# Routed expert blocks: one scatter of whole rows per block, or two scatters of half the columns each

## The chip, the core and the metric

The kernel runs on one core of a Trainium2 chip. Its engines are TensorE (PE in the profile, with its weight loads as PEld), VectorE (DVE), ScalarE (ACT), GpSimd (POOL) and SyncE (SP); data moves by 16 DMA engines that all of them share. The metric is the device time of one execution in microseconds; smaller is better. Everything is float32.

## The reference

One decoder layer on x (4 sequences of 512 tokens, 512 wide): a state-space mixer, attention over a context, and a mixture of experts, each behind a layer norm and added to x. The change lies in the last part:

```python
def _L0_ffn_ref(hidden_states, gate_w, expert_bias, ...):   # E = 16 experts, F = 256, K = 2
    x = hidden_states.reshape(-1, h)
    scores = jax.nn.sigmoid(x @ gate_w)
    _, selected = jax.lax.top_k(scores + expert_bias[None, :], K)
    top_scores = jnp.take_along_axis(scores, selected, axis=1)
    top_scores = top_scores / (top_scores.sum(-1, keepdims=True) + 1e-20)
    shared = jax.nn.silu(x @ shared_gate_w) * (x @ shared_up_w) @ shared_down_w
    comb = jnp.zeros((T, E)).at[jnp.arange(T)[:, None], selected].add(top_scores)
    for e in range(E):
        g, u = jnp.split(x @ experts_gate_up[e], 2, axis=-1)
        routed = routed + comb[:, e:e + 1] * (jax.nn.silu(g) * u @ experts_down[e])
    return (shared + routed).reshape(b, s, h)

x = x + _L0_attn_ref(_layernorm(x), ...)
x = x + _L0_xattn_ref(_layernorm(x), ctx_512, ctx_512)
x = x + _L0_ffn_ref(_layernorm(x), ...)
```

## The kernel before

**Up to 1175 us.** The mixer of one sequence and the attention of another are interleaved on TensorE, and the shared expert and the routing of the first three sequences are computed beside the attention of the last. What is left at the end of the attention is the last sequence's norm, its router and the rest of the shared expert. Each 128-token tile of `x + shared` is stored to `out` (`out_x` in the profile, 2176 rows of 512: 2048 tokens and 128 spare rows); the normed tokens go to a DRAM tile `h_d`.

**The routing's result.** `tables()` (L1180 on) makes a table of blocks. Every expert's chosen tokens are cut into blocks of 128 slots; a block belongs to one expert. For block k, `row_i[:, k]` holds the token's row in `h_d` and in `out` for each of the 128 slots (a spare row for an empty slot), and `wslot[:, k]` the token's weight. The last step before it is returned is L1208, `row_i = none - 1`, from a float tile `none` that holds the row plus 1.

**The routed blocks.** `blocks(0, NB_FEW)` runs 42 blocks (`NB_FEW` = 42; five more stand behind a branch and are not needed for these inputs). TensorE's and SyncE's order is as written; the other engines' instructions are ordered by the framework, each engine in order. For each block:

- `gather(k)` (L1340): GpSimd issues an indirect DMA that fetches the 128 rows of `h_d` into one of four places in `res`, as soon as the transposes of the block that had the place before are done.
- `turn_in` (L1350, L1352): four transposes on TensorE, copied by VectorE to `xT`.
- `up` (L1358, L1363, L1365): eight matmul rows in the profile against the expert's gate and up weights, silu on ScalarE, product `actb` on VectorE.
- `turn_act` (L1371, L1373): two transposes, copied by ScalarE to `aT`.
- `down` (L1379, L1384, L1385): four matmul rows into a PSUM bank `pob`, VectorE scales it with `wslot` into `y` (128 x 512, one of three buffers), and GpSimd issues an indirect DMA that adds the 128 rows of `y` to `out` (`compute_op=ALU.add`: each row is read, added and written by the DMA).

In the emitted order on TensorE a block's `down` comes after the next block's `up` and `turn_in`.

**What orders the scatters.** Two blocks may add to the same row of `out` (a token has two experts), so the framework makes each scatter wait for the landing of the one before: GpSimd waits on that DMA's semaphore ahead of the instruction. On GpSimd, in this order: scatter of block k, gather of block k+7, scatter of block k+1 (the first seven gathers stand ahead of the first scatter). `no_dep` tells the framework that two instructions which seem to touch the same memory need no order.

**The expert weights.** A ring of five places (`ring`, `NW` = 5) holds the weights of five experts, 1.5 MB each. Five are loaded before the blocks begin; `load_later` (L1285) fetches the next one when a place is free and skips the load if the next block needs no new expert. All is issued by SyncE on its own DMA queue; gathers and scatters are on GpSimd's queue.

Of the kernel before, what the change touches and what calls it, by code (L numbers as in the profile page):

```python
# [11 lines left out]
I32 = mybir.dt.int32  # L12
AF = mybir.ActivationFunctionType
ALU = mybir.AluOpType
# [3 lines left out]
P = 128  # L18
B, L, D = 4, 512, 512
# [15 lines left out]
NB = 2 * NT + E - 1  # L35
# [4 lines left out]
ROWS = B * L + P  # L40
# [8 lines left out]
def decoder_layer(ctx: ExitStack, tc: tile.TileContext, a: dict, out: bass.AP):  # L49
    nc = tc.nc  # L50
# [61 lines left out]
    def bank(name, shape=(P, L)):  # L112
        return p_mm.tile(list(shape), F32, tag="mm", name=name)
# [103 lines left out]
    for s in range(SC):  # L217
        base = s * P
        nc.gpsimd.affine_select(
            out=hsel[:, s], in_=hsel[:, s], compare_op=ALU.is_ge, fill=0.0,  # L220
# [3 lines left out]
            out=hsel[:, s], in_=hsel[:, s], compare_op=ALU.is_ge, fill=0.0,  # L224
# [255 lines left out]
    ap = att_pools.enter_context(tc.tile_pool(name="att_1", bufs=1))  # L480
# [344 lines left out]
    def wide(t, shape):  # L825
        return t.unsqueeze(2).to_broadcast(shape)

    def hot_of(g):

        return res[:, 2 * g : 2 * g + 2, :].rearrange("p j (c s) -> p (j c) s", s=P)  # L830
# [261 lines left out]
    with ExitStack() as ph:  # L1092
        ph.enter_context(tc.manual_schedule(engines={ENG.SP}))
        rp = ph.enter_context(tc.tile_pool(name="route", bufs=1))
# [8 lines left out]
        def some(us):  # L1103
            while us > 0 and rest:
                t = next(rest[0], 0)
                lag.step(dve=99.0)
                if t == 0:
                    rest.pop(0)
                elif t is not None:
                    us -= t  # L1110
# [69 lines left out]
        def tables():  # L1180

            pt = p_tr.tile([P, 2, NB], F32, tag="tr", name="ptab")
            n = 2 * TB
            flat = [P, n, NB]
            for g in range(NG):
                val = fs.tile([P, n, 2, NB], F32, tag="val", name=f"val{g}")
                blk = fs.tile(flat, F32, tag="blk", name=f"blk{g}")
                nc.vector.tensor_tensor(
                    blk, rowblk.unsqueeze(1).to_broadcast(flat), wide(rt["high"][:, g], flat),
                    ALU.is_equal,  # L1190
                )
                for m, x in enumerate((ids, rt["wgt"])):
                    x = x[:, g].rearrange("p k t -> p (k t)")
                    nc.vector.tensor_tensor(val[:, :, m, :], blk, wide(x, flat), ALU.mult)
                for t in range(n):
                    nc.tensor.matmul(
                        pt.rearrange("p a k -> p (a k)"), lhsT=hot_of(g)[:, t, :],
                        rhs=val[:, t].rearrange("p a k -> p (a k)"),
                        start=(g == 0 and t == 0), stop=(g == NG - 1 and t == n - 1),
                    )  # L1200
            wslot = rp.tile([P, NB], F32, name="wslot")
            nc.scalar.copy(wslot, pt[:, 1, :])

            none = rp.tile([P, NB], F32, name="none")
            nc.vector.tensor_single_scalar(none, pt[:, 0, :], 0.5, op=ALU.is_lt)
            nc.vector.scalar_tensor_tensor(none, none, spare, pt[:, 0, :], ALU.mult, ALU.add)
            row_i = rp.tile([P, NB], I32, name="row_i")
            nc.vector.tensor_scalar_add(row_i, none, -1.0)  # L1208
            return row_i, wslot

        def runs(eblk, nblk):

# [55 lines left out]
        def later_runs(first, run, run_of, total):  # L1268


            nxt = rp.tile([P, NB], F32, name="next")
            nc.vector.tensor_scalar_add(nxt, run, float(NW))
            row_i = expert_rows(run_of, nxt, NB, "later")
            some_ = rp.tile([P, NB], F32, name="some")
            nc.vector.tensor_tensor(some_, nxt, total.to_broadcast([P, NB]), ALU.is_le)
            cond = rp.tile([P, NB - 1], I32, name="cond")
            nc.vector.tensor_mul(cond, some_[:, : NB - 1], first[:, 1:])
            return cond, row_i
# [4 lines left out]
        def load(k, cond, row, at):  # L1283

            loads[k] = nc.sync.dma_start(  # L1285
                out=wts[:, at].rearrange("p (c w) -> p c w", w=WCP)[:, :, :WC],
                in_=a["experts"][bass.ds(row, P), :].rearrange("p (c w) -> p c w", w=WC),
                cond=cond,
            )


            for n in loads:
                if n != k:
                    no_dep(loads[k], loads[n])
# [13 lines left out]
                bass.ds(value(place, k, (NW - 1) * WR), WR),  # L1308
            )

        def no_dep(later, earlier):
            tc.declare_no_dep(
                later.ins, earlier.ins, reason="another place of the ring, or ordered by PE"
            )

        def weight(k, c):
            return wts[:, bass.ds(places[k] + c * WCP, WC)]
# [7 lines left out]
        def weigh(k, mm):  # L1325

            for n in loads:
                if n > k - NW:  # L1330
                    no_dep(mm, loads[n])
            tc.add_manual_dep(
                mm.ins, loads[k - NW].ins.name,
                mybir.DependencyInfo(mybir.DependencyClass.Sync, mybir.DependencyReason.DATA),
                reason="the block's weights",
            )
# [31 lines left out]
        def turn_act(k, act):  # L1368
# [4 lines left out]
            nc.scalar.copy(aT, pt)  # L1373
            return aT

        def down(k, aT):
            po = bank(f"pob{k}", (P, D))
            for f in range(FC):
                weigh(k, nc.tensor.matmul(  # L1379
                    po, lhsT=aT[:, f, :], rhs=weight(k, DC + f),  # L1380
                    start=(f == 0), stop=(f == FC - 1),
                ))
            y = fs.tile([P, D], F32, tag="y", bufs=3, name=f"y{k}")
            nc.vector.tensor_scalar_mul(y, po, wslot[:, k : k + 1])  # L1384
            nc.gpsimd.indirect_dma_start(  # L1385
                out=out,
                out_offset=bass.IndirectOffsetOnAxis(ap=row_i[:, k : k + 1], axis=0),
                in_=y, in_offset=None, bounds_check=ROWS - 1, compute_op=ALU.add,
            )

        some(6.0)
        pl = p_l.tile([P, TB, E], F32, tag="l", name="pl3")
# [15 lines left out]
        begin, place, parts = runs(eblk, nblk)  # L1408
        for k in range(NW):
            load_ahead(k)  # L1410
        at_once(share(T1, NT) + hot(NG - 1))
        some(10.0)
        row_i, wslot = tables()
        later = later_runs(*parts)
        xgs = {k: gather(k) for k in range(3)}
        some(999.0)

        def blocks(lo, hi):

            for k in range(lo, min(lo + 2, hi)):  # L1420
                locate(k)
            xT = turn_in(lo, xgs.pop(lo))
            aT = None
            for k in range(lo, hi):
                act = up(k, xT)
                if k + 1 < hi:
                    xT = turn_in(k + 1, xgs.pop(k + 1))
                if k + 3 < hi:
                    xgs[k + 3] = gather(k + 3)
                if k > lo:  # L1430
                    down(k - 1, aT)
                    if k - 1 + NW < hi:
                        load_later(k - 1)
                aT = turn_act(k, act)
                if k + 2 < hi:
                    locate(k + 2)
            down(hi - 1, aT)
# [76 lines left out]
```

## Time and profile before

| what | value |
|---|---|
| median of 3 runs | 1445.25 us (1443.98 to 1445.43) |
| the profiled execution | 1448.94 us |
| its span, first to last instruction | 1446.9 us |
| mean granted TensorE clock | 0.968 |
| PE busy | 1361.7 us (94%) |
| POOL busy | 302.3 us (21%) |
| scatter, L1385 | 42 times, 1573 ns on GpSimd each |
| gather, L1340 | 42 times, 1056 ns on GpSimd each |
| GpSimd's queue | 9408 packets, 22.03 MB |

Busy time of an engine is the time in its instructions; an indirect DMA's time on GpSimd is that of making its descriptors, not that of moving the data. The page's second part cuts the span in 40 slices of 36 us; a digit is a busy share in tenths. The routed blocks are the last eight of them:

```
PE   6999999999999999999999999999998899999891
POOL 4024000311210032121011103213000034343442
DMA  9000000000000000000000200001001546677753
```

"Idle before, releaser" names what an engine waited for just before an instruction; where several semaphores were waited for, the one that came last by the profile. Chain views follow the last instruction back through what released it.

### The profile page before, as it was taken

What the parts mean: (1) busy time and instruction counts of PE and PEld (TensorE: products, weight loads), DVE (VectorE), ACT (ScalarE), POOL (GpSimd) and SP (SyncE); (2) the same over time, 40 slices, a digit from 0 to 9 for tenths busy, and PEclk for the clock granted to TensorE, in tenths of its full rate; (3) what the DMA queues carried; (4) which work ended last, traced back from release to release, by engine and by line L of the source; (5) the groups of instructions that cost most, each with busy time, mean ns of one, the idle gap of its engine ahead of it and who ended that gap; (6) DMA issues with size and microseconds to landing.
All of it is one profiled execution on the core that took longest, in us unless ns stands there. A gap on an engine that the chain in (4) does not pass through costs nothing. (4 is left out here: it accounts for less than half of the span.)

```text
span 1446.9 us, 15750 instructions
## 1 busy us (share of the span) xinstructions
PE 1361.7 (94%) x5776; PEld 533.1 (37%) x5776; DVE 695.0 (48%) x1026; ACT 494.1 (34%) x652; POOL 302.3 (21%) x342
## 2 busy tenths in 40 slices
PE   6999999999999999999999999999998899999891
PEld 3444333333333333333333332333334544444440
DVE  4452656554566654456665444554573623322220
ACT  3221334533644443354443334455443011111110
POOL 4024000311210032121011103213000034343442
PEclk9999999999999999989999998999997799999996
DMA  9000000000000000000000200001001546677753
GB/s 355 27 1 0 0 5 4 4 7 6 4 12 4 4 7 6 4 4 5 4 21 11 64 5 26 25 24 37 33 1 73 214 119 154 137 175 221 195 85 39
DMA packets 40925, 76.82 MB, mean 53 GB/s; under 512 B 5393, under 2 KB 8977, under 8 KB 40593
## 3 DMA queue, kind: packets, MB, share of 16 engines
q1 hardware_dynamic: 30576, 53.24, 10.7%
q0 software_dynamic: 9408, 22.03, 8.0%
q8 instruction: 48, 0.79, 0.2%
q10 hardware_dynamic: 864, 0.55, 0.1%
q14 instruction: 29, 0.23, 0.0%
HBM read 96.76 MB, written 19.92 MB: 81 GB/s over the span
## 5 line engine op out<-in xcount | busy, mean ns | idle before, releaser
L551 DVE TENSOR_REDUCE qp<-pm 128x2 f32<-128x1024 f32 x256 | 313.5, 1225 | 342.2 <-PE pw L562 326.4
L566 ACT ACTIVATE ex<-pw 128x1024 f32<-128x1024 f32 x256 | 261.9, 1023 | 393.5 <-PE pw L562 392.7
L545 PE MATMUL pm<-kt,qTq 16*128 16x512 f32 x1024 | 288.9, 643 | 15.8 <-DVE qp L551 14.0
L562 PE MATMUL pw<-qTm,kt 17*128 17x512 f32 x1024 | 291.2, 645 | 3.7 <-ACT ex L566 3.7
L1358 PE MATMUL pgb<-ring,xT 128*128 x336 | 153.4, 600 | 2.8 <-DVE xT L1352 2.8
L100 POOL TENSOR_SCALAR qp<-res,mvq,rstdq 128x64 f32<-128x64 f32 x128 | 71.8, 580 | 401.3 <-PE ptm L533 347.8
L545 PEld LDWEIGHTS pm<-kt,qTq 16*128 16x128 f32 x1024 | 76.5, 183 | 191.5 <-DVE qp L551 102.7
L571 PE MATMUL pav<-ex,va 128*32 128x512 f32 x1024 | 139.0, 615 | 0.1
L311 PE MATMUL px<-xnT,ssm_large 128*128 128x512 f32 x256 | 126.3, 630 | 0.0
L456 PE MATMUL po<-ssm_large 128*128 128x512 f32 x256 | 121.7, 606 | 0.0
L311 PE MATMUL pz<-xnT,ssm_large 128*128 128x512 f32 x256 | 121.0, 607 | 0.0
L1385 POOL DMA_INDIRECT out_x<-y,row_i x42 | 66.1, 1573 | 138.5 <-DMA out_x<-y,row_i 85.4
L1358 PEld LDWEIGHTS pgb<-ring,xT 128*128 128x128 f32 x336 | 61.1, 192 | 65.3 <-issue 61.4
L562 PEld LDWEIGHTS pw<-qTm,kt 17*128 17x128 f32 x1024 | 77.0, 184 | 12.9 <-ACT ex L566 8.8
L1379 PE MATMUL pob<-ring,aT 128*128 x168 | 79.1, 593 | 0.5 <-ACT aT L1373 0.5
L1384 DVE TENSOR_SCALAR y<-pob,wslot 128x512 f32<-128x512 f32 x42 | 31.5, 751 | 98.2 <-DMA out_x<-y,row_i 64.7
L311 PEld LDWEIGHTS px<-xnT,ssm_large 128*128 128x128 f32 x256 | 47.1, 197 | 77.2 <-issue 76.2
L368 DVE SCALAR_TENSOR_TENSOR xc<-px,wcv,xc 128x511 f32<-128x511 f32 (+2 forms) x96 | 71.7, 747 | 5.7 <-ACT xc L364 3.5
L311 PEld LDWEIGHTS pz<-xnT,ssm_large 128*128 128x128 f32 x256 | 45.1, 189 | 68.4 <-issue 67.7
L590 POOL TENSOR_TENSOR res<-res,o 128x256 f32<-128x256 f32 x32 | 23.3, 727 | 214.8 <-DVE o L586 213.3
L456 PEld LDWEIGHTS po<-ssm_large 128*128 128x128 f32 x256 | 44.6, 189 | 63.7 <-issue 62.9
L1340 POOL DMA_INDIRECT res<-h_d,row_i x42 | 44.4, 1056 | 86.1 <-DVE row_i L1208 53.9
(213 smaller groups left out, 1308.5 us busy)
## 6 DMA issues: line engine op xcount, KB each, us to landing
ring<-in_experts SPq DMA_DIRECT2D x42, 1536.0 KB
kt<-in_ctx_t SPq DMA_DIRECT2D x128, 32.0 KB
h_d<-hn SPq DMA_DIRECT2D x16, 256.0 KB
out_x<-res SPq DMA_DIRECT2D x16, 256.0 KB
res<-in_x SPq DMA_DIRECT2D x3, 1024.0 KB
ssm_large<-in_w_in SPq DMA_DIRECT2D x2, 1024.0 KB
ssm_large<-in_w_out SPq DMA_DIRECT2D x1, 2048.0 KB
ssm_large<-in_w_in SPq DMA_DIRECT2D x6, 256.0 KB
```

What stands on the lines that cost most here:

```text
L100: eng.tensor_scalar(dst, src, mv[:, j, 0:1], rstd[:, j : j + 1], ALU.subtract, ALU.mult)
L311: nc.tensor.matmul(pm, lhsT=win[:, piece, c, :], rhs=xnT[:, c, :], start=(c == 0), stop=(c == DC - 1),)
L368: nc.vector.scalar_tensor_tensor(xc[:, d:], px[:, : L - d], wcv[:, i, KW - 1 - d : KW - d], xc[:, d:], ALU.mult, ALU.add,)
L456: nc.tensor.matmul(po, lhsT=zg[:, i, ts(j, P)], rhs=wout[:, i, :], start=(i == 0), stop=(i == IC - 1),)
L545: nc.tensor.matmul(ps[:, g - g0, :], lhsT=qT[g * SL : g * SL + HD, ts(j, P)], rhs=kts[i % NQ][g * SL : g * SL + HD, :], start=True, stop=True,
L551: nc.vector.tensor_reduce(qps[i % NQ][:, j, g0 : g0 + 2, HD], ps, AX.X, ALU.max, negate=True)
L562: nc.tensor.matmul(ps[:, g - g0, :], lhsT=kts[i % NQ][rows, ts(c, P)], rhs=qT[rows, :], start=True, stop=True,)
L566: nc.scalar.activation(ex[:, g0 : g0 + 2, :], ps, AF.Exp, scale=1.0 / HD**0.5)
L571: nc.tensor.matmul(pav[ts(g, SL), :], lhsT=vas[b % 2][:, c, v, :], rhs=ex[:, g, :], start=(c == 0), stop=(c == TB - 1),)
L1358: weigh(k, nc.tensor.matmul(pg, lhsT=xT[:, c, :], rhs=weight(k, c), start=(c == 0), stop=(c == DC - 1),))
L1379: weigh(k, nc.tensor.matmul(po, lhsT=aT[:, f, :], rhs=weight(k, DC + f), start=(f == 0), stop=(f == FC - 1),))
L1385: nc.gpsimd.indirect_dma_start(out=out, out_offset=bass.IndirectOffsetOnAxis(ap=row_i[:, k : k + 1], axis=0), in_=y, in_offset=None, bound ...
```

## The change

Each block's scatter becomes two: the first adds columns 0 to 255 of `y`, the second columns 256 to 511. `out` is seen as 4352 rows of 256 for it, where row r's halves are rows 2r and 2r + 1. `half_i` holds these row numbers; it is made in `tables()` from `none` by two more VectorE instructions. `row_i` stays for the gathers. The framework is told that a first half and a second half never touch the same bytes, so each half waits for the earlier scatter of the same half alone. The order on GpSimd is that of before with two scatters in the place of one; VectorE has the two instructions for `half_i` behind row_i's; on the other engines the order of the instructions is the same.

```diff
@@ tables()
             row_i = rp.tile([P, NB], I32, name="row_i")
             nc.vector.tensor_scalar_add(row_i, none, -1.0)
-            return row_i, wslot
+
+            half_i = rp.tile([P, 2, NB], I32, name="half_i")
+            for h in range(2):
+                nc.vector.tensor_scalar(
+                    half_i[:, h], none, 2.0, float(h - 2), ALU.mult, ALU.add
+                )
+            return row_i, half_i, wslot
@@ no_dep()
-        def no_dep(later, earlier):
-            tc.declare_no_dep(
-                later.ins, earlier.ins, reason="another place of the ring, or ordered by PE"
-            )
+        def no_dep(later, earlier, reason="another place of the ring, or ordered by PE"):
+            tc.declare_no_dep(later.ins, earlier.ins, reason=reason)
@@ down()
+        out_halves = out.rearrange("r (h c) -> (r h) c", h=2)
+        scattered = [], []
+
         def down(k, aT):
...
             y = fs.tile([P, D], F32, tag="y", bufs=3, name=f"y{k}")
             nc.vector.tensor_scalar_mul(y, po, wslot[:, k : k + 1])
-            nc.gpsimd.indirect_dma_start(
-                out=out,
-                out_offset=bass.IndirectOffsetOnAxis(ap=row_i[:, k : k + 1], axis=0),
-                in_=y, in_offset=None, bounds_check=ROWS - 1, compute_op=ALU.add,
-            )
+            for h in range(2):
+                add = nc.gpsimd.indirect_dma_start(
+                    out=out_halves,
+                    out_offset=bass.IndirectOffsetOnAxis(ap=half_i[:, h, k : k + 1], axis=0),
+                    in_=y[:, ts(h, D // 2)], in_offset=None, bounds_check=2 * ROWS - 1,
+                    compute_op=ALU.add,
+                )
+                for other in scattered[1 - h]:
+                    no_dep(add, other, "other columns")
+                scattered[h].append(add)
@@ the call
-        row_i, wslot = tables()
+        row_i, half_i, wslot = tables()
```

## The prediction

> **What bounds the kernel now.** I read the page first (PE busy 94% of the span), then the chain that ended last, then the timeline of TensorE and of GpSimd over the routed blocks (1175 to 1441 us), the scatter's line, and the busy times by stretches.
>
> The chain that ended last is short and has no TensorE in it. Its columns are start, duration, what:
>
> ```profile
> 1430.27 4.74 DMA out_x<-y,row_i
> 1435.01 0.02 issue
> ...
> 1435.05 0.51 issue
> ...
> 1435.78 1.54 POOL out_x L1385
> ```
>
> A scatter issued at 1430.27 lands 4.74 us later, and 0.76 us after that the next is issued. One accumulating scatter waits for the landing of the one before: at the end the kernel runs at the pace of that chain, one block in 5.5 us. The records of the DMA's semaphores put the last landing at 1440.60; the remaining 6.3 us to the span's end are the closing of the program and are not touched.
>
> The same line's view over all 42 blocks:
>
> ```profile
>   DMA out_x<-y,row_i: 85.4, 24
> ...
> who waited for it (us, times):
>   POOL out_x L1385: 85.4, 24
>   DVE y L1384: 64.7, 15
> ...
> DMA to landing us min/median/max: 4.7/4.9/8.6
> ```
>
> GpSimd waits for earlier scatters, and VectorE waits for them too, because y has three buffers and block k's y needs block k-3's scatter to have landed.
>
> TensorE (start, duration, the four matmuls of `down` as one row):
>
> ```profile
> 1268.25 1.88 PE L1379 MATMUL pob<-ring,aT 128*128 x4
> 1274.06 1.88 PE L1379 MATMUL pob<-ring,aT 128*128 x4
> ...
> 1343.94 1.88 PE L1379 MATMUL pob<-ring,aT 128*128 x4
> ...
> 1350.99 1.88 PE L1379 MATMUL pob<-ring,aT 128*128 x4
> ...
> 1360.04 1.88 PE L1379 MATMUL pob<-ring,aT 128*128 x4
> ```
>
> Free of waits a block takes TensorE 5.81 us (1274.06 - 1268.25). Late in the phase it is held: steps of 7.05 and 9.05 here, 6.78 at 1372.63 and two of 5.9 before, together 5.6 us over the pace, through VectorE waiting for y's buffer. TensorE's last `pob` ends at 1417.46, so without those holds at 1411.85. The last scatter starts at 1435.77: 24 us behind what TensorE could allow.
>
> GpSimd (start, duration, idle before it and its releaser):
>
> ```profile
> 1157.79 1.02 POOL L1340 DMA_INDIRECT res<-h_d,row_i  x1 [0.30 <-issue]
> ...
> 1290.65 1.57 POOL L1385 DMA_INDIRECT out_x<-y,row_i  x1 [2.63 <-DMA out_x<-y,row_i]
> 1292.53 1.06 POOL L1340 DMA_INDIRECT res<-h_d,row_i  x1 [0.30 <-issue]
> 1296.42 1.58 POOL L1385 DMA_INDIRECT out_x<-y,row_i  x1 [2.83 <-DMA out_x<-y,row_i]
> 1298.31 1.06 POOL L1340 DMA_INDIRECT res<-h_d,row_i  x1 [0.30 <-issue]
> 1304.60 1.57 POOL L1385 DMA_INDIRECT out_x<-y,row_i  x1 [5.23 <-DVE xT L1352]
> ```
>
> Scatter to scatter is 5.77, then 8.18. From the first scatter (1178.24) to the last are 257.5 us in 41 steps. The first five follow TensorE (5.81); ten steps are long (7.04 to 9.39, 80.3 us in all); the other 26 average 5.70, which is the 4.9 landing plus 0.81 from landing to issue. The long ones, 2.33 over 5.70 each, meet a load of expert weights (1.5 MB on the same 16 DMA engines):
>
> ```profile
> 1295.00:1303.00 8.00, 8.00 (x26) 3.88 (x25) 1.77 (x3) 0.88 (x3) 2.63 (x2) 1.00 0.98 283
> 1303.00:1306.00 3.00, 3.00 (x12) 1.52 (x11) 1.77 (x3) 0.63 (x2) 1.40 (x1) 1.00 0.09 33
> 1306.00:1319.00 13.00, 13.00 (x41) 6.35 (x40) 2.80 (x5) 1.51 (x4) 3.86 (x4) 1.00 1.00 314
> ```
>
> (last columns: granted clock 1.00, DMA share, GB/s.) The DMA share jumps to 0.98 and 1.00 with the loads. There are 11 such loads after 1206 in the DMA records. So the chain gains only 0.11 us a block on TensorE, loses 2.33 at each long step, and never catches up.
>
> **The change part by part.** *Added on VectorE:* two instructions for `half_i`, of row_i's form (182 ns): 0.36 us. They stand behind row_i, which the first gather waits for, and the first scatter comes 22 us later; cover: the shared-expert work TensorE still does then. Taken as 0, bounds 0 and 0.4. The first block's TensorE work is the late one if the cover is gone.
>
> *Doubled on GpSimd:* 42 more indirect DMAs of 128 rows. The descriptors are per row, and the two forms of 128 rows take 1.06 (gather) and 1.57 (scatter, accumulating); the half is a scatter, so 1.57, bounds 1.06 and 1.8. Queued behind a half are the other half, then the next gather. Back to back gaps are 0.30 (the gathers above). A block then needs 1.57 + 0.30 + 1.57 + 0.30 + 1.06 + 0.30 = 5.10 us of GpSimd, up from 3.23 busy and gap, and stays below TensorE's 5.81. The gather behind block k's scatter is for block k+7 and finds its place free about four blocks (23 us) before its transposes, and TensorE waited for a gather only once, 0.2 us, with the chain 24 us behind: some us more cost nothing.
>
> *The wait itself:* a first half waits for the first half before it only, likewise the second. Each chain's step is landing + 0.81, and the other half and the gather are issued inside that wait. So the gain is not from the two chains as such: both halves of a block still have to go round at landing + 0.81. What counts is how much sooner half a row lands. In the packet records the last scatter has 128 packets of 2048 B, eight for each DMA engine, 158 ns apart. A gather's packets have 4096 B and take 159 ns, and an accumulating packet reads its source and its destination, 2 x 2048 B: the spacing goes with bytes. Half the bytes save at most 8 x 79 ns = 0.63, at least 0 if all of it is latency; I take 0.5, near the byte end. Landing 4.4, step 5.21, 0.60 below TensorE's 5.81. (The Trainium skill, "DMA: Bandwidth & Descriptors", section "Anatomy of one DMA — SWDGE (gpsimd) path", gives about 2.0 us fixed and 1 us for 436 KB, so 131 KB less would save an estimated 0.30 us; the trace's fixed part is longer than its 2.0. By it the step would be 5.41.)
>
> *Loads:* in the step from 1207.30 no packet of the scatter moved before 1212.0, while load packets ran from 1207.9: mostly waiting, which half the bytes do not shorten, and two halves cover more of the time, so every one of 11 loads should hit. I take 2.6 us each; bounds 1.2 (half the old cost) and 3.7 (the longest step, 9.39 - 5.70).
>
> **Sum.** How far the chain is behind TensorE, block by block: each block -0.60, not below 0; a block with a load +2.0 (5.21 + 2.6 - 5.81). Loads at blocks 5, 8, 13, 16, 19, 20, 21, 24, 25, 26, 28. Behind after block 5: 2.0; 8: 2.8; 13: 2.4; 16: 3.2; 21: 8.0; 28: 14.2; then 12 blocks at -0.60: 7.0; the last block follows TensorE's short last step (2.72): +2.5 = 9.5. At 14.2 VectorE's wait for y's buffer is under 1 us, so TensorE is no longer held: its end is 1411.85. From pob's end to the scatter is 1.1 (1206.22 to 1207.30). Last first half: 1411.85 + 1.1 + 9.5 = 1422.45; second half 1.87 later, 1424.3; landed at 1428.7, against 1440.60: -12 us. The profiled execution took 1448.94 (span 1446.9), the median of the runs is 1445.25; the difference is applied to the median: 1433.
>
> **The rivals.**
> *A. TensorE becomes the bound.* A load costs a pair half as much, 1.2. Then a load adds 0.6, the chain is 0 behind by block 32 and ends only 2.5 behind: 1421.7 landed, -19: 1426. For it: fewer bytes per half. Against: the idle start in 1207.9 to 1212.0.
> *B. The landing shortens by 0.3 only.* Per packet part of the 158 ns is fixed. Step 5.41, -0.40 a block, +2.2 a load: 19.0 behind after block 28, 14.2 after 40, 16.9 at the end, landed at 1436.3: -4: 1441.
> *C. Slower: half a row lands as late as a whole one.* The place is GpSimd's wait for the earlier half. If landing stays at 4.9, the step stays 5.70, each block's end moves back by the second half's 1.87, and 11 loads at 2.6 against ten at 2.33 add 5.3: +1.9 to +7.2, middle 1450. It decides from a landing of about 4.7 (36 lagging blocks x 0.2 = 7.2). For it: 3.25 of the 4.8 us come after GpSimd's part, and the unloaded gather, half that traffic on the engines, still needs 3.4. Against: the byte-paced packets. (The Trainium skill's same page, section "Rules for kernel authors", says two transfers to disjoint partition halves are not worth it, as they serialize on the same engines; here it is columns, and no run yet shows which.)
> *D. GpSimd becomes the bound.* If the 0.51 us of issue before a waiting scatter does not overlap the instruction before it, a block costs 1.57 x 2 + 1.06 + 0.81 x 2 + 0.30 = 6.12, 36 x 0.42 = 15 us more: 1460. Against: the 0.30 gaps, the next one being prepared while one runs.
> That the chains stay tied is a fifth way, folded into C: in the built program a second half waits for the second half before it and for a DMA eight issues back, long landed, so I see no tie.
>
> **Chances.** Forecast 0.36, A 0.11, B 0.20, C 0.26, D 0.07. Within 0.2% (2.9 us, about what repeats can tell) falls some of B (0.07) and C (0.04). Faster 0.36 + 0.11 + 0.13 = 0.60, same 0.11, slower 0.22 + 0.07 = 0.29. Range: A's 1426 less a us below, C's upper end 1452 above: 1425 to 1452; D and the tails are left out. The likeliest case alone: 1427 to 1440 (a load at 1.5 to 3.2).
>
> **What would show it.** Right: halves of 1.57 us on GpSimd with 0.30 between them, landing median near 4.4, steps of first half to first half about 5.2 where no load runs, no TensorE wait for actb or xT after 1340, last pob near 1412. Wrong: landing at 4.7 or more (C), gaps of 0.8 inside a pair (D), GpSimd idle until y at most blocks (A), or a load delaying both halves in turn, more than 3.2 a time.

## The result, and the profile after

| what | before | after |
|---|---|---|
| median of 4 runs | 1445.34 us (1443.98 to 1448.96) | 1430.42 us (1430.00 to 1430.77) |
| the profiled execution | 1448.94 us | 1430.26 us |
| its span | 1446.9 us | 1428.4 us |
| POOL busy | 302.3 us | 369.0 us |
| packets on GpSimd's queue | 9408 | 15456 |

The ratio is 0.9893 with a 95% interval of 0.9875 to 0.9911: 14.9 us faster by the medians. The two profiled spans differ by 18.5 us, and not all of that is the change: TensorE's first `pob` ends at 1177.17 before and at 1174.92 after. These 2.25 us arise ahead of the routed blocks: from 850 to 900 us, where both kernels run the same instructions, the profile has a mean granted clock of 0.90 before and 0.97 after. The kernel before without loads (below) has 0.90 there too, so whether this goes with the change or with the execution is open. The closing after the last landing takes 6.3 and 5.5 us. From the first `pob` to the last landing it is 263.4 us before (1440.60 - 1177.17) and 248.0 after (1422.92 - 1174.92; the landings are from the records of the DMAs' semaphores): 15.4 us less. This phase is what the account below explains.

The scatter's line after, all 84 halves (idle time of GpSimd before them and its releaser; who waited for them; time to landing):

```profile
  DMA out_x<-y,half_i: 35.1, 17
...
  POOL out_x L1395: 35.1, 17
  DVE y L1391: 19.1, 7
...
DMA to landing us min/median/max: 3.8/3.9/7.9
```

GpSimd's wait for earlier scatters fell from 85.4 to 35.1 us, VectorE's for y's buffer from 64.7 to 19.1, the median landing from 4.9 to 3.9 (3.86 over all 84 halves in the semaphore records).

GpSimd after, around two weight loads (start, duration, idle before and its releaser):

```profile
1289.31 1.58 POOL L1395 DMA_INDIRECT out_x<-y,half_i  x1 [0.31 <-issue]
1291.19 1.55 POOL L1395 DMA_INDIRECT out_x<-y,half_i  x1 [0.30 <-issue]
1293.05 1.10 POOL L1344 DMA_INDIRECT res<-h_d,row_i  x1 [0.30 <-issue]
1294.45 1.58 POOL L1395 DMA_INDIRECT out_x<-y,half_i  x1 [0.31 <-issue]
1299.86 1.55 POOL L1395 DMA_INDIRECT out_x<-y,half_i  x1 [3.83 <-DMA out_x<-y,half_i]
1301.71 1.09 POOL L1344 DMA_INDIRECT res<-h_d,row_i  x1 [0.30 <-issue]
1303.11 1.58 POOL L1395 DMA_INDIRECT out_x<-y,half_i  x1 [0.31 <-issue]
```

Two halves and a gather follow each other with 0.30 us between them, 5.14 us in all (1289.31 to 1294.45): where the chain is behind TensorE, no load runs and gathers are still being issued, GpSimd does not wait for a landing, and its own instructions set the step. With a load running the second half waits 3.83 us, and that step is 8.66 (1294.45 to 1303.11).

TensorE after has one wait left from 1180 us on, the last block's own:

```profile
PE pob L1386 <- ACT aT L1377: 0.5, 1, 0.5
```

The end, from the chain that ended last (start, duration, what):

```profile
1407.49 4.42 DMA out_x<-y,half_i
...
1412.67 3.77 DMA out_x<-y,half_i
1416.44 0.03 issue
1416.48 0.50 issue
...
1417.20 1.30 POOL out_x L1395
```

It still ends in a chain of landings. TensorE's last `pob` ended at 1409.60, the last first half starts at 1417.20: 6.5 us later than the 1.1 us that the way through `y` takes. Before, the last scatter started 18.3 us after TensorE's end, which itself had been held up 5.6 us.

### The profile page after: what moved, and what is told of

It is laid out like the page before. It is cut to its first block, busy times and chain, and to the rows that moved or that the text cites. A ratio compares the mean times of both kernels' runs of the same rounds, so it can differ in the third digit from the quotient of the medians.

```text
span 1428.4 us, 15839 instructions
## 1 busy us (share of the span) xinstructions
PE 1356.9 (95%) x5776; PEld 533.0 (37%) x5776; DVE 696.1 (49%) x1028; ACT 494.0 (35%) x652; POOL 369.0 (26%) x384
## 3 DMA queue, kind: packets, MB, share of 16 engines
q0 software_dynamic: 15456, 22.03, 9.0%
## 4 chain that ended last, share of the span: by engine, by line
PE 86%; DVE 7%; ACT 2%; DMA 2%; issue 1%; POOL 1%; POOLq 0%; SPq 0%; DVEq 0%; ACTq 0%
PE pm L545 17%; PE pgb L1362 10%; PE pz L311 8%; PE po L456 8%; PE pav L571 8%; PE px L311 7%; PE pob L1386 4%; DVE qp L551 4%; PE pd L311 2%; PE pb L311 2%; PE pc L311 2%; PE pi L444 2%; PE pe L714 2%; PE pg L686 2%; PE pw L562 2%; DMA out_x<-y,half_i 1%
## 5 line engine op out<-in xcount | busy, mean ns | idle before, releaser
L1395 POOL DMA_INDIRECT out_x<-y,half_i x84 | 131.5, 1565 | 65.6 <-DMA out_x<-y,half_i 35.1
L1369 DVE TENSOR_TENSOR actb<-pgb,sgb 128x256 f32<-128x256 f32 x42 | 17.8, 425 | 130.1 <-ACT sgb L1367 126.8
```

What stands on the lines that cost most here:

```text
L1395: add = nc.gpsimd.indirect_dma_start(out=out_halves, out_offset=bass.IndirectOffsetOnAxis(ap=half_i[:, h, k : k + 1], axis=0), in_=y[:, ts ...
```

## The experiments

**The two waits beside each other.** The halves stay, in one chain:

```diff
-                for other in scattered[1 - h]:
-                    no_dep(add, other, "other columns")
-                scattered[h].append(add)
```

> The halves stay, but the second half waits for the first and the next first half for the second: one chain of 84 half scatters. Theory (the gain needs the two waits to run beside each other; a half lands 3.86 us after its issue and the next starts 0.8 later): a block takes 2 x 4.67 = 9.34 us on the chain, 41 x 9.34 = 383 us from 1176 us on, with some load delays about 1590 to 1610 us in all. Rival (what helped is that half a row lands sooner, and the two chains add nothing): near the changed kernel, 1430 to 1440.

Measured: 1582.52 us, one run, 7.5 us under the range expected; before on the same chip 1449.21. GpSimd near the end:

```profile
1510.95 1.55 POOL L1395 DMA_INDIRECT out_x<-y,half_i  x1 [2.60 <-DMA out_x<-y,half_i]
1512.81 1.10 POOL L1344 DMA_INDIRECT res<-h_d,row_i  x1 [0.30 <-issue]
1515.52 1.58 POOL L1395 DMA_INDIRECT out_x<-y,half_i  x1 [1.61 <-DMA out_x<-y,half_i]
1519.74 1.55 POOL L1395 DMA_INDIRECT out_x<-y,half_i  x1 [2.64 <-DMA out_x<-y,half_i]
```

Each half waits; second half to second half is 8.8 us, a little under the 9.34 expected because the waiting half starts 0.26 or 0.76 us after the landing, mostly in turn, and not 0.8 always. A sooner landing alone gives nothing if a block needs two of them in a row; the separate chains are worth some 150 us against this kernel.

**What the second half costs.** It is not scattered (columns 256 to 511 of the output lack the routed part):

```diff
-            for h in range(2):
+            for h in range(1):
                 add = nc.gpsimd.indirect_dma_start(
```

> The second half is not scattered, so columns 256 to 511 of the output lack the routed part; one chain of 42 half scatters. Theory (in the changed kernel GpSimd's 5.14 us per block sets the step where no load runs, and the second half costs its 1.87 us in that step): the step falls to landing 3.86 + 0.81 = 4.67, the chain catches up 1.14 us a block instead of 0.67 and has caught up at the end: about 1424. Rival (the second half is hidden in the wait of the first, the landing sets the step): 1428 to 1431, as the changed kernel less its last second half.

Measured: 1423.88 us (1423.50 to 1429.70), ratio to before 0.9837 (0.9805 to 0.9870). GpSimd between loads:

```profile
1367.85 1.57 POOL L1395 DMA_INDIRECT out_x<-y,half_i  x1 [1.76 <-DMA out_x<-y,half_i]
1369.73 1.06 POOL L1344 DMA_INDIRECT res<-h_d,row_i  x1 [0.30 <-PE ptg L1354]
1372.48 1.57 POOL L1395 DMA_INDIRECT out_x<-y,half_i  x1 [1.70 <-DVE y L1391]
```

The step is 4.63 us, landing plus 0.81, and GpSimd idles 1.7 in it. So the second half is not hidden: it makes 4.63 into 5.14. Its price is 6.5 us of the whole by the medians, its bytes on the DMA engines and its place behind the last first half included.

**What the loads do to each chain.** In both kernels the condition of every later weight load is 0 (blocks of the later experts use other experts' weights):

```diff
-            nc.vector.tensor_mul(cond, some_[:, : NB - 1], first[:, 1:])
+            nc.vector.tensor_single_scalar(cond, some_[:, : NB - 1], 2.0, op=ALU.is_ge)
```

> The changed kernel with the condition of every later weight load set to 0, so that blocks of the later experts use the weights of the first five (their part of the output is another). Theory (the chain falls behind TensorE only through the 11 loads, about 3.2 us each): the last first half starts 2.9 us after TensorE's end instead of 7.6, about 1426. Rival (the chain is the bound all the way, loads or not): 1429 to 1431.

> The kernel before with the condition of every later weight load set to 0 (blocks of the later experts use the weights of the first five). Theory (the old chain's step of 5.70 keeps up with TensorE's 5.81 as long as no load runs; what the change improves is the catching up after loads): the whole gain is gone, 1425 to 1428, within 2 us of the changed kernel without loads. Rival (the old chain lags for its landing alone): 1436 to 1445, still 10 us or more above the changed kernel without loads.

Measured: 1426.03 us (1425.47 to 1426.94) after, 1428.84 us (1426.54 to 1432.55) before; ratios to the kernel before 0.9841 (0.9815 to 0.9867) and 0.9859 (0.9827 to 0.9891), which overlap. The old scatter without loads:

```profile
  DVE y L1384: 70.1, 40
  DMA out_x<-y,row_i: 8.2, 2
...
DMA to landing us min/median/max: 4.5/4.9/5.0
```

It waits for y 40 times and for a landing twice: it keeps TensorE's pace. From TensorE's last `pob` to the last landing the profiles show 8.8 us after (1409.19 to 1417.96) and 9.5 before (1411.95 to 1421.49). The median of before lies 0.8 us above the range expected and 2.8 us above the other, with runs that overlap; TensorE's first `pob` ends 2.8 us earlier in the profile of after (1174.5 against 1177.3), ahead of the routed blocks. From the first `pob` to the last landing it is 243.5 us after and 244.2 before. Of the phase's 15.4 us only 0.8 are left: the old chain is not too slow for TensorE, it is too slow to catch up after a load.

**More, smaller pieces.** Four chains of 128 columns (the row numbers and the list of scatters without order follow suit):

```diff
-        scattered = [], []
+        scattered = [], [], [], []
...
-            for h in range(2):
+            for h in range(4):
...
-                    in_=y[:, ts(h, D // 2)], in_offset=None, bounds_check=2 * ROWS - 1,
+                    in_=y[:, ts(h, D // 4)], in_offset=None, bounds_check=4 * ROWS - 1,
...
```

> Four scatters of 128 columns each in four chains. Theory (GpSimd's time to make descriptors goes by rows, not bytes, and is the floor of the step): a block takes 4 x 1.87 + 1.36 = 8.84 us on GpSimd, landing about 3.4, so loads are absorbed and the phase takes 41 x 8.84 less the missing gathers at the end: about 1545 us. Rival (the landing sets the step, shorter landings are what helps): 1425 to 1430.

Measured: 1550.86 us, one run; before 1446.08. GpSimd at the end:

```profile
1524.80 1.55 POOL L1395 DMA_INDIRECT out_x<-y,half_i  x1 [0.30 <-issue]
1526.66 1.55 POOL L1395 DMA_INDIRECT out_x<-y,half_i  x1 [0.30 <-issue]
1528.52 1.55 POOL L1395 DMA_INDIRECT out_x<-y,half_i  x1 [0.30 <-issue]
1530.38 1.55 POOL L1395 DMA_INDIRECT out_x<-y,half_i  x1 [0.30 <-issue]
```

A quarter takes GpSimd as long as a half or a whole (1.55), although it lands in 3.34 us (median of the 168 in the semaphore records). GpSimd is the bound from the first block on, at 8.87 us each as long as gathers are issued. Splitting pays only while all pieces and the gather stay below TensorE's 5.81.

**Three pieces per weight load, at once or spread.** Each later load becomes three DMAs of two weight chunks, either one after the other or one in each of three successive blocks (`load_rest` issues piece 1 of the load one block back and piece 2 of the load two back):

```diff
+            load(k, value(later[0], k, 1), *of[k], 0, 2)
...
+        def load_rest(k):
+            for n in (k - 1, k - 2):
+                if n in of and len(loads[n]) == k - n:
+                    load(n, value(later[0], n, 1), *of[n], 2 * (k - n), 2)
...
                     if k - 1 + NW < hi:
                         load_later(k - 1)
+                    load_rest(k - 1)
```

> Each later weight load is cut into three DMAs of 512 KB, issued one after the other. Theory (the scatters are held by the load's bytes queued on the same DMA engines): no change from the changed kernel, 1428 to 1433. Rival (one large DMA holds the engines until it is through, smaller ones let the scatters in between): 1425 to 1428.

> The same three DMAs of 512 KB, one in each of three successive blocks. Theory (a load costs the chain 3.2 us because 1.5 MB come in one burst; a third of it costs about 1 us, which the slack of 5.14 against TensorE's 5.81 and of 4.67 against 5.14 takes up within a block): nearly as without loads, 1425 to 1428. Rival (the delay is one of each load's start, not of its bytes, so it comes three times as often): 1434 or more.

Measured: at once 1428.47 us (1425.69 to 1431.66), ratio 0.9860 (0.9822 to 0.9897). That lies across both expectations and does not tell them apart. Spread 1443.46 us (1440.23 to 1447.79), ratio 0.9973 (0.9956 to 0.9991): the theory's time was missed by 15 us or more, and the rival's number was met. Its reason was not. The scatters at the end, spread:

```profile
1424.58 1.55 POOL L1407 DMA_INDIRECT out_x<-y,half_i  x1 [2.40 <-DVE y L1403]
1426.44 1.55 POOL L1407 DMA_INDIRECT out_x<-y,half_i  x1 [0.31 <-issue]
1429.95 1.55 POOL L1407 DMA_INDIRECT out_x<-y,half_i  x1 [1.96 <-DVE y L1403]
...
1434.69 1.55 POOL L1407 DMA_INDIRECT out_x<-y,half_i  x1 [1.33 <-DMA out_x<-y,half_i]
```

They wait for y: the chain is not behind. TensorE's last `pob` ends at 1431.60, 22 us later than in the changed kernel, and the last first half follows 3.1 us after it, as without loads. TensorE's waits, spread, and one of them with the blocks around it:

```profile
PE pgb L1374 <- DMA ring<-in_experts: 7.3, 4, 3.3
PE pgb L1374 <- issue: 4.9, 4, 2.5
...
1314.18 5.37 PE L1374 MATMUL pgb<-ring,xT 128*128 x8 [1.89 <-issue]
...
1321.76 3.60 PE L1374 MATMUL pgb<-ring,xT 128*128 x8
```

The wait moved to TensorE, which now meets weights that are not there. Block k waits for the last piece of the load five blocks earlier, whether that load ran or was skipped, and spread over three blocks this piece is issued two blocks later. The lateness itself is not the whole of the 22 us. The waits at `pgb` come to 12.8 us, 4.9 of them under `issue`, where the profile names no releaser. Three groups of eight matmuls right behind such a wait take 5.37, 6.69 and 5.37 us where the others take 3.60, 6.6 us together, and the profile's granted clock there is 0.50 (1315.3 to 1318.7, 1356.3 to 1363.1 and 1380.2 to 1383.6). That the skipped loads' pieces are behind the waits under `issue` is argued, not shown. The profiled execution is also the slowest of the ten.

**Gathers out of the way.** Twelve places in `res` instead of four, gathers eight blocks earlier:

```diff
-            xg = res[:, 2 * TB + k % TB, :]
+            xg = res[:, (2 * TB + k % (3 * TB)) % (3 * TB), :]
...
-        xgs = {k: gather(k) for k in range(3)}
+        xgs = {k: gather(k) for k in range(11)}
...
-                if k + 3 < hi:
-                    xgs[k + 3] = gather(k + 3)
+                if k + 11 < hi:
+                    xgs[k + 11] = gather(k + 11)
...
```

> The gathers get twelve places in place of four and are issued eight blocks earlier, so that GpSimd has none in the last 14 blocks. Theory (GpSimd's 5.14 us per block, of which a gather is 1.36, sets the speed of catching up): the last blocks step at landing + 0.76 = 4.6 and gain 1.2 us each on TensorE instead of 0.67, which takes the 6 us at the end away: 1425 to 1427. Rival (the landing sets the step): 1430, as the changed kernel.

Measured: 1427.57 us (1426.54 to 1428.83), ratio 0.9850 (0.9817 to 0.9883). GpSimd late in the phase:

```profile
1374.84 1.55 POOL L1395 DMA_INDIRECT out_x<-y,half_i  x1 [1.23 <-DMA out_x<-y,half_i]
1376.70 1.55 POOL L1395 DMA_INDIRECT out_x<-y,half_i  x1 [0.30 <-issue]
1379.48 1.55 POOL L1395 DMA_INDIRECT out_x<-y,half_i  x1 [1.23 <-DVE xT L1356]
```

Without gathers the step is 4.64: the 5.14 was GpSimd's. The time is above the 1425 to 1427 hoped for by half a microsecond.

**Together, beside the changed kernel.** Four kernels in one series, five rounds; the last spreads a load over two blocks, 768 KB in each, with the earlier gathers:

```diff
+            load(k, value(later[0], k, 1), *of[k], 0, 3)
...
+        def load_rest(k):
+            if k - 1 in of and len(loads[k - 1]) == 1:
+                load(k - 1, value(later[0], k - 1, 1), *of[k - 1], 3, 3)
```

> The changed kernel once more, beside the three that follow, on the same chip: 1430 us, 1428 to 1432.

> The changed kernel with the gathers issued eight blocks earlier, once more. Theory (GpSimd sets the speed of catching up): 2 to 4 us below the changed kernel. Rival: within 1 us of it.

> Gathers issued earlier and each weight load in three DMAs at once. Theory (a load's bytes cost the delay, however they are cut): as the kernel with the earlier gathers alone, within 1 us. Rival (smaller loads let the scatters through): 2 us or more below it.

> Gathers issued earlier and each weight load in two DMAs of 768 KB in two successive blocks. Theory (spreading takes the delay off the scatters, and TensorE waits for late weights only where the last piece comes two blocks late, as it did with three pieces): 1425 to 1427. Rival (one block late is too late as well): 1432 or more, with TensorE waiting for ring.

| kernel | median us | runs | ratio to before (interval) |
|---|---|---|---|
| changed | 1431.23 | 1430.28 to 1437.49 | 0.9910 (0.9887 to 0.9933) |
| + gathers earlier | 1428.30 | 1425.53 to 1431.74 | 0.9886 (0.9863 to 0.9909) |
| + loads in three pieces at once | 1426.39 | 1424.65 to 1431.37 | 0.9879 (0.9855 to 0.9902) |
| + loads over two blocks | 1425.24 | 1424.66 to 1425.53 | 0.9860 (0.9838 to 0.9882) |

The earlier gathers are 2.9 us below the changed kernel by the medians, as expected, though the intervals overlap. Pieces at once against whole loads stay undecided. The two-block version has the lowest median of those that compute everything: all its runs lie below all runs of the changed kernel, 6 us by the medians. Its scatters:

```profile
  DMA out_x<-y,half_i: 39.1, 22
  DVE y L1401: 18.2, 15
...
DMA to landing us min/median/max: 3.6/3.8/7.6
```

Its last first half starts 3.0 us after TensorE's end (1409.01 to 1411.99), as in the kernel without loads (1409.19 to 1412.32). TensorE waits for no weights in it, so one block later is in time here and two were not.

What spreading adds to the earlier gathers is not shown. The intervals of the last three kernels overlap, and from the first `pob` to the last landing their profiles take 243.5, 243.4 and 243.2 us, against 248.4 in the changed kernel's second profile and 243.5 without loads: in these executions the earlier gathers alone had caught up at the end. They do not always: the last first half starts 3.2 us after TensorE's end in this profile of that kernel (1409.59 to 1412.80) and 5.0 in the one of the series before (1411.01 to 1416.00). What can be said is that the two-block version's five runs lie within 1 us of each other and the earlier gathers' six spread over 6.

## Why the prediction was right, step by step

The direction, the bound and the way of the gain were right. The size came out in part by luck: the landing was taken half a microsecond too long, and another limit, which stood close by, hid most of it.

*The bound of before* (a chain of landings that falls behind at loads and does not recover): shown. Without loads the old chain keeps up, and the gain goes.

*The step of 5.21.* The number held (5.14), its reason did not. The prediction took it as landing 4.4 plus 0.81, with GpSimd's 5.10 just below it. The landing is 3.86, so landing plus 0.81 is 4.67 and GpSimd sets the step. This is the term that was mis-sized: the saving per half was put at 0.5, with 0.63 as the most that packet spacing could give, and it is 1.05. That the step came out near 5.21 all the same is luck: GpSimd's floor, which the prediction had at 5.10 as a thing that stays out of the way, caught it.

*Loads, 2.6 each over 11.* In the chain of first halves nine steps lie between 7.16 and 9.13, 27.6 us over 5.14 together, and two of 5.79 and 5.91 add 1.4: 29.0 over 11 loads, 2.6 each. The kernel's second profile gives 31.3, or 2.8 each. (In the packet records of the step from 1207.30, load packets run from 1207.75 and the scatter's first packet comes at 1212.30; the prediction had 1207.9 and 1212.0, which changes nothing.)

*The sum.* Behind at its most: 14.2 forecast, 13.3 measured. Behind at the end: 9.5 forecast, 6.5 measured. The last six blocks have no gather on GpSimd; their steps are 4.51 to 5.18, 27.9 us together where six of 5.21 would be 31.3. With the landing taken too long the prediction could not see that GpSimd's relief there counts. That and the last landing (0.5) make the 15.4 us of the phase out of the forecast 11.9; the median moved by 14.9 where 12 was forecast.

*TensorE no longer held:* shown, one wait of 0.5 us is left. One size on the way was too small: VectorE's wait for `y`'s buffer was to be under 1 us and is up to 3.7, in seven waits of 19.1 us together, but none of them reaches TensorE.

*The rivals.* A (TensorE the bound, 1426) is wrong for the changed kernel; the two-block version ends as it describes. B and C fell with the landing: at 0.3 or nothing saved they would have held, and it is 1.05. The Trainium skill's figure ("DMA: Bandwidth & Descriptors", section "Anatomy of one DMA — SWDGE (gpsimd) path") gave an estimated 0.30 and was too small by more than three times for these accumulating scatters, which saved 1.05; the measurement decides. The same page of the Trainium skill advises against splitting (section "Rules for kernel authors"), but speaks of disjoint partition halves, which no run here tried; for column halves of a chain of dependent scatters two pieces pay and four do not. D's mechanism (0.51 us of issue unhidden) did not appear, the gaps are 0.30; but GpSimd as the bound is what remains of it, at 5.14 instead of 6.12, and the quarters show it in full.

*half_i for nothing:* the profile gives no sign of a cost. From `row_i`'s start to the first gather's it is 0.49 us in both kernels (1153.45 to 1153.94 after, 1155.72 to 1156.21 before), and from the first gather's start to the end of TensorE's first `down` it is 21.0 us in both kernels (1153.9 to 1174.9 after, 1156.2 to 1177.2 before).

## What to carry to other kernels

A chain that keeps pace on average can still set the end: what counts is its margin for catching up after each disturbance, here 0.11 us a block before and 0.67 after. Splitting a dependent transfer into independent chains pays if each piece lands sooner and the issuing engine's fixed cost for all pieces stays below the pace that must be kept. After that, look for what else stands in that engine's queue: issuing the gathers earlier was worth some 3 us here by the medians, with intervals that overlap. Spreading the bursts on the shared DMA engines can make their own users late, as three blocks did; what it is worth in two blocks is not settled here.

## What was not expected of the hardware

The landing of an accumulating scatter of 128 rows is close to linear in its bytes: 4.91 us for 256 KB, 3.86 for 128 KB, 3.34 for 64 KB, about 2.8 us plus 2.1 per 256 KB. The packets of one engine follow each other after 158 ns at 2048 B and 82 ns at 1024 B, which explains some 0.6 us of the 1.05; the rest lies in the first packets, up to 1.1 us long in the whole scatter's records and up to 0.7 in the half's. Why these shorten too, no run here tells. GpSimd's time for such a scatter does not depend on the bytes at all: 1.55 to 1.58 us at the median in each of the three sizes.
